# Second bias of the experts in two row tiles of TensorE, its rows loaded per tile, and silu placed before the next first layer

## The chip, the cores and the metric

The kernel runs on one core of a Trainium2 chip. The time is the device time of one execution in microseconds (us); smaller is better. Three runs of the kernel before took 1146.60, 1147.37 and 1149.48 us, so the median is 1147.37 us. A core has a matrix engine (TensorE, "PE" in the profile, with its weight loads as "PEld"), VectorE (DVE), ScalarE (ACT), GpSimd (POOL) and SyncE (SP), which only starts transfers here. Each has its own queue of instructions and they meet through semaphores. PE reads from SBUF and writes to PSUM, from which DVE and ACT fetch results.

## The reference

A layernorm, two graph layers over 1250 nodes and 40000 edges, a second layernorm, and then a layer of 8 experts of which each token uses two. Only this last part is touched by the change. Cut to it:

```python
# t: 1250 x 1024; D, H, E, K = 1024, 256, 8, 2
logits = silu(t @ rw1 + rb1) @ rw2 + rb2
vals, idx = top_k(logits, K)
w = softmax(logits with all but those K set to -inf)
eh = silu(einsum('td,edh->teh', t, ew1) + eb1)
eo = einsum('teh,ehd->ted', eh, ew2) + eb2      # eb2: 8 x 1024
y = t + einsum('te,ted->td', w, eo)
```

The second bias is eb2: for each expert a row of 1024 numbers that is added to every token's output of that expert.

## The kernel before

The kernel first does the graph layers (`gnn_windows`), then routing and experts (`moe`). A check of the edges decides at the end whether a general version has to run; with these inputs it doesn't.

In `moe` the tokens are sorted by expert into tiles of 128 rows. There can be up to 27 tiles; with these inputs there are 23. The list `eid` says which expert a tile belongs to, `ids` which tokens it holds, `to` where its rows are added, and `w_slot` the weight of each row. The first four tiles are planned from the first eight blocks of tokens (`plan_first`), the rest later (`plan_rest`), and the expert work of tiles 0 to 3 runs beside that second planning. All experts' weights lie in SBUF (`xw`), and an expert is picked by a register as an index.

One tile i goes through these steps:

- `gather(i)` (L1493): GpSimd fetches the 128 token rows from DRAM into one of three buffers by an indirect transfer.
- `fetch(i)` (L1504, L1505): PE turns the tile in eight 128 x 128 transposes, four to one PSUM buffer of the pool `tpp`; ScalarE copies each buffer of four to SBUF. The pool has two buffers.
- `first_layer(i, xT)` (L1516, L1521): eight float32 matmuls give 128 x 256 hidden values in PSUM; each shows as two passes in the profile. VectorE copies them to `hx`. Here the expert's number is also read into registers of PE and ScalarE.
- `second_layer(i, e, hx)`: two transposes turn `hx` (L1528, into a `tpp` buffer), ScalarE adds the first bias and applies silu to each half (L1530), and then each half of the 1024 output columns gets its own PSUM buffer of the pool `mm2`: a bias matmul (L1537), then two float32 matmuls (L1541, again two passes each). ScalarE scales the first half by the row weights (L1547), VectorE the second (L1549). GpSimd then adds the rows to `out` in DRAM by an indirect transfer (L1552), called the scatter below.

The bias matmul multiplies a 3 x 128 matrix of ones (`ones_b`, bfloat16) by 3 x 512 numbers: eb2 was split into three bfloat16 parts whose sum is the float32 value, and the parts were stored in DRAM as `eb2_d` of 3 x 8192. Before the experts begin, ScalarE's queue loads all of it once into three partitions of the buffer `WW` (L1624), and the matmul picks the expert's columns by PE's register.

`section(i0, i1)` sets the order in which the program is written for a run of tiles: for each i, the gather of tile i + 3, the fetch of tile i + 1, the first layer of tile i, then the second layer of tile i - 1. A planner then orders each engine's instructions: it keeps dependencies, takes instructions in program order where they are ready by its own model of times, and otherwise lets later ones that are ready go first. What `tc.keep_in_program_order` wraps is not moved that way. Tiles 0 to 19 exist always; from tile 20 on the work stands in `If` blocks that compare the number of tiles, and `sections` finishes the last tile that is held.

In `add_logits` (L1112) the router's last small matmuls already use `tile_position`: four of them with 32 columns each take four column tiles of the array.

Of the kernel before, what the change touches and what calls it, by code (L numbers as in the profile page):

```python
# [10 lines left out]
F32 = mybir.dt.float32  # L11
F32R = mybir.dt.float32r
F16 = mybir.dt.float16
BF = mybir.dt.bfloat16
# [5 lines left out]
ENG = mybir.EngineType  # L20

P = 128
# [3 lines left out]
LQ = 32  # L26
# [3 lines left out]
def kernel(  # L30
# [21 lines left out]
    nc = tc.nc  # L52
    N, D = x.shape
    NE = src.shape[0]
    E, _, H = ew1.shape
    KD = D // P
    KH = H // P
    HALF = D // 2
# [21 lines left out]
    const = ctx.enter_context(tc.tile_pool(name="const", bufs=1))  # L80
# [6 lines left out]
    eb2_d = dram.tile([3, E * D], BF, name="eb2_d")  # L87
# [7 lines left out]
    WW = L[:, NT + 4 * D :]  # L95
# [171 lines left out]
    def routing_constants():  # L267
        late = tc.keep_in_program_order
        tiles = counted(tiles_i, "tiles")
        token = counted(token_i, "token")  # L270
        own_row = counted(own_row_i, "own_row")
        first = counted(first_i, "first")
        late(nc.vector.tensor_scalar(first, first, 0.0, None, op0=ALU.is_gt))

        lower = const.tile([P, P], F16, name="lower")
        late(nc.vector.tensor_scalar(lower, lane, own_row, None, op0=ALU.is_gt))
        ones = const.tile([P, P], F16, name="ones")
        late(nc.vector.memset(ones, 1.0))
        valid = const.tile([P, NB], F32, name="valid")
        late(nc.vector.tensor_scalar(valid, token, float(N), None, op0=ALU.is_lt))  # L280

        late(nc.vector.tensor_scalar(token, token, 1.0, None, op0=ALU.add))
        late(nc.vector.tensor_mul(token, token, valid))
        rb1_p = const.tile([P, KD], F32, name="rb1_p")
        late(nc.sync.dma_start(out=rb1_p, in_=rb1.rearrange("(k p) -> p k", p=P)))

        rb2_p = const.tile([P, 1], F32, name="rb2_p")
        late(nc.vector.memset(rb2_p, 0.0))
        late(nc.sync.dma_start(out=rb2_p[:E], in_=rb2.rearrange("(e o) -> e o", o=1)))
        eb1_p = const.tile([P, E, KH], F32, name="eb1_p")  # L290
        late(nc.sync.dma_start(out=eb1_p, in_=eb1.rearrange("e (k p) -> p e k", p=P)))
        rw2_sb = const.tile([P, KD, LQ], F32, name="rw2_sb")
        late(nc.vector.memset(rw2_sb, 0.0))
        late(nc.sync.dma_start(out=rw2_sb[:, :, :E], in_=rw2.rearrange("(k p) e -> p k e", p=P)))

        ev = L[: E * D // P, NT - 320 : NT]
        eb2_f = ev[:, :P]
        late(nc.sync.dma_start(out=eb2_f, in_=eb2.rearrange("e (a n) -> (e a) n", n=P)))
        for i in range(3):
            part = ev[:, P + i * (P // 2) : P + (i + 1) * (P // 2)].bitcast(BF)  # L300
            late(nc.vector.tensor_copy(part, eb2_f))
            if i < 2:
                late(nc.vector.tensor_tensor(eb2_f, eb2_f, part, ALU.subtract))
            late(nc.sync.dma_start(out=eb2_d[i].rearrange("(a n) -> a n", n=P), in_=part))
        ones_b = const.tile([3, P], BF, name="ones_b")
        late(nc.vector.memset(ones_b, 1.0))
        lg = const.tile([P, NB, E], F32, name="lg")
        late(nc.vector.memset(lg, 0.0))
        need.update(
            tiles=tiles, token=token, first=first, lower=lower, ones=ones, valid=valid,  # L310
            rb1_p=rb1_p, rb2_p=rb2_p, eb1_p=eb1_p, rw2_sb=rw2_sb, ones_b=ones_b, lg=lg,
        )
# [698 lines left out]
    def moe():  # L1011
# [4 lines left out]
        rb1_p, rb2_p, eb1_p, rw2_sb, ones_b, lg = (  # L1016
            need[k] for k in ("rb1_p", "rb2_p", "eb1_p", "rw2_sb", "ones_b", "lg")
        )
# [71 lines left out]
        ids, to, eid = (keep([P, NTILE], I32) for _ in range(3))  # L1090
# [395 lines left out]

        w1_all = xw.rearrange("p (e w) -> p e w", e=E)[:, :, : KD * H]
        w2_all = xw.rearrange("p (e w) -> p e w", e=E)[:, :, KD * H :]
        eb2_r = WW.bitcast(BF)[:3, : E * D]
        eb2_e = eb2_r.rearrange("i (e d) -> i e d", e=E)  # L1490

        def gather(i):
            nc.gpsimd.indirect_dma_start(  # L1493
# [4 lines left out]
        def fetch(i):  # L1498
            xg = xgs[i % 3]
            xT = xTb[i % 2]  # L1500
            for q in range(0, KD, 4):
                pt = tpp.tile([P, 4, P], F32, name="tp")
                for k in range(4):
                    nc.tensor.transpose(pt[:, k, :], xg[:, (q + k) * P : (q + k + 1) * P], ident)  # L1504
                nc.scalar.copy(xT[:, q : q + 4, :], pt)  # L1505
            return xT

        def first_layer(i, xT):
            e = nc.values_load(
                eid[0:1, i : i + 1], engines=(ENG.PE, ENG.Activation),  # L1510
                min_val=0, max_val=E - 1,
                skip_runtime_bounds_check_because="eid is a count of experts, cut at E - 1",
            )
            ps = mm.tile([P, 512], F32, name="ps")
            for k in range(KD):
                nc.tensor.matmul(  # L1516
                    ps[:, :H], xT[:, k, :], w1_all[:, ds(e, 1), k * H : (k + 1) * H],
                    start=(k == 0), stop=(k == KD - 1),
                )
            hx = hxs[i % 2]  # L1520
            nc.vector.tensor_copy(hx, ps[:, :H])  # L1521
            return e, hx

        def second_layer(i, e, hx):
            pt = tpp.tile([P, 4, P], F32, name="tp")
            hT = hTs[i % 2]
            for q in range(KH):
                nc.tensor.transpose(pt[:, q, :], hx[:, q * P : (q + 1) * P], ident)  # L1528
            for q in range(KH):
                nc.scalar.activation(  # L1530
                    hT[:, q, :], pt[:, q, :], AF.Silu, bias=eb1_p[:, ds(e, 1), q : q + 1]
                )
            yo = yos[i % 2]
            for h in range(2):
                dc = slice(h * HALF, (h + 1) * HALF)
                ps = mm2.tile([P, 512], F32, name="ps2")
                nc.tensor.matmul(  # L1537
                    ps, ones_b, eb2_e[:, ds(e, 1), dc], start=True, stop=False
                )
                for q in range(KH):  # L1540
                    nc.tensor.matmul(  # L1541
                        ps, hT[:, q, :],
                        w2_all[:, ds(e, 1), q * D + h * HALF : q * D + (h + 1) * HALF],
                        start=False, stop=(q == KH - 1),
                    )
                if h == 0:
                    nc.scalar.activation(yo[:, dc], ps, AF.Copy, scale=w_slot[:, i : i + 1])  # L1547
                else:
                    nc.vector.tensor_scalar(  # L1549
                        yo[:, dc], ps, w_slot[:, i : i + 1], None, op0=ALU.mult  # L1550
                    )
            nc.gpsimd.indirect_dma_start(  # L1552
                out=out[:, :],
                out_offset=bass.IndirectOffsetOnAxis(ap=to[:, i : i + 1], axis=0),
                in_=yo, in_offset=None, bounds_check=N - 1, oob_is_err=False,
                compute_op=ALU.add,
            )
# [6 lines left out]
        xTs, held = {}, {}  # L1564

        def section(i0, i1, joined=True, until=None):
            for i in range(i0, i1):
                if i + 3 < NTILE and i > 1:
                    gather(i + 3)
                if i + 1 < (until or i1):  # L1570
                    xTs[i + 1] = fetch(i + 1)
                held[i] = first_layer(i, xTs.pop(i))
                if i > i0 or joined:
                    second_layer(i - 1, *held.pop(i - 1))

        def sections(i0, ends):
            last = held.pop(i0 - 1)
            if not ends:
                second_layer(i0 - 1, *last)
                return  # L1580

            joined = i0 == always
            if not joined:
                second_layer(i0 - 1, *last)
            with tc.If(n_tiles > i0) as more:
                xTs[i0] = fetch(i0)
                if joined:
                    held[i0 - 1] = last
                section(i0, ends[0], joined)
                sections(ends[0], ends[1:])  # L1590
            if joined:
                with more.Else():
                    second_layer(i0 - 1, *last)


        w0, w1 = route_w.pop(0), route_w.pop(0)
# [24 lines left out]
        logits(LAST)  # L1621
        lgp.close()
        mm2 = st.enter_context(tc.tile_pool(name="mmy", bufs=3, space=PSUM))
        nc.scalar.dma_start(out=eb2_r, in_=eb2_d[:, :])  # L1624
        xTs[0] = fetch(0)
        xTs[1] = fetch(1)
        held[0] = first_layer(0, xTs.pop(0))
# [14 lines left out]

    gnn_windows()
    ok = moe()
    with tc.If(ok == 0):
        gnn_any()
        moe()
# [34 lines left out]
```

## Time and profile before

The profiled execution took 1146.48 us, and its span from the first to the last instruction is 1144.3 us. The granted TensorE clock is 0.993 on average.

| What | Number | Where |
|---|---|---|
| PE busy in 958 to 1080 us | 122.00 of 122.00 us | busy time by stretch |
| ScalarE, VectorE, GpSimd busy there | 33.63, 16.46, 36.01 us | same |
| DMA engines' busy share there | 0.53 | same |
| L1516, one pass of the first layer | 384 ns, 368 of them | costliest groups |
| L1541, one pass of the second layer | 597 ns, 184 of them | same |
| L1537, one bias matmul | 379 ns, 46 of them | that line's instructions |
| L1530, silu of one half | 364 ns, 46 of them | same |
| L1505, copy of four transposes | 586 ns, 46 of them | same |
| L1552, scatter: issue to landing | 4.6 / 6.0 / 7.1 us (least, median, most) | same |

A record of a matmul lasts longer than the array is occupied[...]; the step from one start to the next is what counts. "PEld" with an idle time in brackets is a weight load that came later than the one before ended; after "<-" stands what is thought to have released it, and "issue" means that the profile shows no cause.

### The profile page before, as it was taken

To read this page: it belongs to the slowest core of one execution; us is meant where nothing else is said; L and a number is where in the kernel's file an instruction comes from. 1 tells how busy PE (TensorE), PEld (TensorE's weight loads), DVE (VectorE), ACT (ScalarE), POOL (GpSimd) and SP (SyncE) were. 2 spreads that over 40 slices of the span, in tenths; PEclk is the share of its full clock that TensorE was granted. 3 is DMA by queue.
4 is the path that set the end of the run, shared out by engine and by line. 5 is a ranking of instruction groups with operands and counts; after the bars stand their busy time and mean duration, and the time that the engine had idled before them with its cause. 6 is when DMAs were issued, how large, how long until landed. Compare 5 with 4: busy or idle time off the path is not lost.

```text
span 1144.3 us, 13214 instructions
## 1 busy us (share of the span) xinstructions
PE 1108.3 (97%) x4775; PEld 791.2 (69%) x4775; DVE 451.1 (39%) x1129; ACT 181.5 (16%) x420; POOL 331.7 (29%) x438
## 2 busy tenths in 40 slices
PE   6999999999999999999999999999999989999994
PEld 4556556888888886887688778885444766666662
DVE  8777777761212154341224132555322542111110
ACT  5301000001111111100110000123011223222220
POOL 1899999800000000032003002342000013223221
PEclk9999999999999999999999999999999999999997
DMA  6110111010100021042004261335921435444542
GB/s 230 34 38 5 38 38 38 1 37 1 38 1 1 1 74 38 1 154 93 7 10 168 88 222 42 117 148 209 373 60 37 150 92 136 112 113 105 127 115 45
DMA packets 59330, 95.40 MB, mean 83 GB/s; under 512 B 8797, under 2 KB 35645, under 8 KB 59251
## 3 DMA queue, kind: packets, MB, share of 16 engines
q1 hardware_dynamic: 48400, 67.72, 17.3%
q0 software_dynamic: 7056, 23.88, 9.2%
q10 hardware_dynamic: 3798, 2.84, 0.8%
q8 instruction: 42, 0.69, 0.2%
q14 instruction: 34, 0.28, 0.1%
HBM read 68.76 MB, written 27.47 MB: 84 GB/s over the span
## 4 chain that ended last, share of the span: by engine, by line
PE 93%; DVE 2%; ACT 1%; DMA 1%; POOL 1%; issue 0%; ACTq 0%; DVEq 0%; POOLq 0%
PE ps L528 12%; PE ps L462 11%; PE psb L642 9%; PE ps L712 8%; PE ps L564 8%; PE ps L642 7%; PE ps L1516 7%; PE ps L1541 7%; PE ps L1188 5%; PE ps L629 5%; PE ps L1202 4%; PE cnt L423 3%; PE tp L1504 2%; PE ps L1141 2%; PE ps L1537 1%; PE tp L322 1%
## 5 line engine op out<-in xcount | busy, mean ns | idle before, releaser
L413 POOL TENSOR_SCALAR ol<-lane,keys 125x128 f16<-125x128 f16 x320 | 193.2, 622 | 27.6 <-DVE oh L420 27.6
L462 PE MATMUL ps<-h0T,L 128*128 128x498 f32 (+2 forms) x384 | 147.4, 518 | 0.2 <-ACT h0T L325 0.2
L528 PE MATMUL ps<-L,h0T 128*128 128x256 f32 (+1 forms) x640 | 142.0, 380 | 0.0
L708 POOL TENSOR_TENSOR L<-L 128x512 f32<-128x512 f32 (+1 forms) x20 | 31.4, 1576 | 375.1 <-DMA L<-in_L_gnn_b_dram 216.5
L528 PEld LDWEIGHTS ps<-L,h0T 128*128 128x128 f32 (+1 forms) x640 | 118.7, 188 | 17.7 <-issue 0.5
L420 DVE TENSOR_SCALAR oh<-win,keys 125x240 f16<-125x240 f16 x320 | 84.7, 322 | 32.7 <-PE cnt L423 31.1
L462 PEld LDWEIGHTS ps<-h0T,L 128*128 128x128 f32 x384 | 68.1, 192 | 38.3 <-issue 33.9
L1516 PE MATMUL ps<-xw,L 128*128 x368 | 84.9, 384 | 0.4 <-issue 0.4
L1541 PE MATMUL ps<-xw,L 128*128 x184 | 83.5, 597 | 0.1
L564 PE MATMUL ps<-C,yh 128*128 128x256 f32 (+2 forms) x240 | 81.9, 356 | 0.0
L564 PE MATMUL ps<-C,yl 128*128 128x256 f32 (+2 forms) x240 | 81.5, 354 | 0.0
L712 PE MATMUL ps<-zh,C 128*128 128x512 f32 (+1 forms) x200 | 79.6, 398 | 0.0
L712 PE MATMUL ps<-zl,C 128*128 128x512 f32 (+1 forms) x200 | 78.7, 393 | 0.0
L1516 PEld LDWEIGHTS ps<-xw,L 128*128 128x128 f32 x368 | 69.2, 193 | 10.3 <-issue 1.8
L1552 POOL DMA_INDIRECT out_dram<-L x23 | 36.3, 1579 | 133.5 <-ACT L L1505 87.9
L442 DVE TENSOR_TENSOR C<-C,cnt 128x240 f32 x160 | 64.3, 402 | 12.5 <-DVE oh L420 1.6
L1493 POOL DMA_INDIRECT L<-t_d,L x26 | 26.0, 1000 | 148.1 <-DVE L L141 127.8
L1541 PEld LDWEIGHTS ps<-xw,L 128*128 128x128 f32 x184 | 33.3, 190 | 35.3 <-issue 32.9
L423 PEld LDWEIGHTS <-ol 125*128 125x128 f16 x320 | 30.9, 97 | 36.7 <-POOL ol L413 20.0
L1549 DVE TENSOR_SCALAR L<-ps,L 128x512 f32<-128x512 f32 x23 | 17.3, 751 | 91.8 <-PE ps L1541 91.8
L394 DVE TENSOR_TENSOR yl<-ps,yh 128x256 fp32r<-128x256 f32 (+1 forms) x40 | 16.9, 424 | 92.1 <-ACT yh L393 92.1
L423 PE MATMUL cnt<-oh,ol 125*128 125x240 f16 x320 | 50.0, 266 | 2.6 <-POOL ol L413 2.1
(226 smaller groups left out, 1504.3 us busy)
## 6 DMA issues: line engine op xcount, KB each, us to landing
xw<-in_L_ffn_ew_dram SPq DMA_DIRECT2D x16, 1024.0 KB, 7.6
L<-in_x_dram SPq DMA_DIRECT2D x20, 256.0 KB, 2.8
v_d<-L SPq DMA_DIRECT2D x18, 256.0 KB, 2.0
xa<-v_d SPq DMA_DIRECT2D x18, 256.0 KB, 6.0
t_d<-L SPq DMA_DIRECT2D x9, 512.0 KB, 4.0
out_dram<-xa SPq DMA_DIRECT2D x9, 512.0 KB, 3.7
L<-in_L_gnn_W_self_dram SPq DMA_DIRECT2D x4, 1024.0 KB, 5.4
L<-in_L_gnn_W_neigh_dram SPq DMA_DIRECT2D x4, 1024.0 KB
```

Of the source, the lines that this page charges most:

```text
L413: nc.gpsimd.tensor_scalar(ol[:, c, :], lane[:GP], keys[:, 1, c, r : r + 1], None, op0=ALU.is_equal)
L420: nc.vector.tensor_scalar(oh, win[:GP], keys[:, 0, i * GC + c, r : r + 1], None, op0=ALU.is_equal)
L423: nc.tensor.matmul(ps[:, i, :GW], ol[:, i * GC + c, :], oh, start=(c == 0), stop=(c == GC - 1),)
L442: nc.vector.tensor_tensor(to, to.bitcast(F32), ps[:, i, :GW].rearrange("p (k w) -> p k w", k=NB), ALU.add,)
L462: nc.tensor.matmul(ps[:, :n], w[:, k, (d % 2) * P : (d % 2 + 1) * P], h0T[:, k, c0 : c0 + n], start=(k == 0), stop=(k == KD - 1),)
L528: nc.tensor.matmul(ps[:m, :QW], hT[:, k, blk(b)], w[:, k, :], start=(k == 0), stop=(k == KD - 1))
L564: nc.tensor.matmul(ps[:, :n], part[: rows[k], k, (d % 2) * P : (d % 2 + 1) * P], C[: rows[k], k, c0 : c0 + n], start=(k == 0 and part is y ...
L629: nc.tensor.matmul(ps[:m], hT1[:, k, blk(b)], w[:, k, :], start=(k == 0), stop=(k == KD - 1))
L642: nc.tensor.matmul(ps, rows_of(k), w[:, k, :], start=(first and k == 0), stop=(k == KB - 1), skip_group_check=not first,)
L712: nc.tensor.matmul(ps[:m], C[: rows[k], k, blk(b)], part[: rows[k], k, :], start=(k == 0 and part is yh), stop=(k == NB - 1 and part is yl),)
L1516: nc.tensor.matmul(ps[:, :H], xT[:, k, :], w1_all[:, ds(e, 1), k * H : (k + 1) * H], start=(k == 0), stop=(k == KD - 1),)
L1541: nc.tensor.matmul(ps, hT[:, q, :], w2_all[:, ds(e, 1), q * D + h * HALF : q * D + (h + 1) * HALF], start=False, stop=(q == KH - 1),)
```

## The change

Three things are done. First, `second_layer` is split: the transposes of the hidden rows and the silus become `turn_hidden`, and `section` writes them ahead of the next tile's first layer. Second, the two bias matmuls of a tile are written one directly after the other, kept in program order, in front of both halves of the second layer, and each gets a row tile of the array: the first has its three rows in partitions 0 to 2, the second in partitions 32 to 34. `LQ` is 32. `ones_b` therefore has 35 partitions. Third, the bias rows are no longer loaded once for all experts. `load_bias(i)` has SyncE read tile i's expert into a register and load its 3 x 512 numbers for each half to one of four fixed places; the matmul then needs no register.

```diff
@@ -302,7 +302,7 @@
             if i < 2:
                 late(nc.vector.tensor_tensor(eb2_f, eb2_f, part, ALU.subtract))
             late(nc.sync.dma_start(out=eb2_d[i].rearrange("(a n) -> a n", n=P), in_=part))
-        ones_b = const.tile([3, P], BF, name="ones_b")
+        ones_b = const.tile([LQ + 3, P], BF, name="ones_b")
         late(nc.vector.memset(ones_b, 1.0))
         lg = const.tile([P, NB, E], F32, name="lg")
         late(nc.vector.memset(lg, 0.0))
@@ -1486,8 +1486,19 @@
 
         w1_all = xw.rearrange("p (e w) -> p e w", e=E)[:, :, : KD * H]
         w2_all = xw.rearrange("p (e w) -> p e w", e=E)[:, :, KD * H :]
-        eb2_r = WW.bitcast(BF)[:3, : E * D]
-        eb2_e = eb2_r.rearrange("i (e d) -> i e d", e=E)
+
+        ebs = [WW.bitcast(BF)[:, i * HALF : (i + 1) * HALF] for i in range(4)]
+
+        def load_bias(i):
+            e = nc.values_load(
+                eid[0:1, i : i + 1], engines=(ENG.SP,), min_val=0, max_val=E - 1,
+                skip_runtime_bounds_check_because="eid is a count of experts, cut at E - 1",
+            )
+            for h in range(2):
+                nc.sync.dma_start(
+                    out=ebs[i % 4][h * LQ : h * LQ + 3],
+                    in_=eb2_d[:, ds(e * D + h * HALF, HALF)],
+                )
 
         def gather(i):
             nc.gpsimd.indirect_dma_start(
@@ -1521,7 +1532,7 @@
             nc.vector.tensor_copy(hx, ps[:, :H])
             return e, hx
 
-        def second_layer(i, e, hx):
+        def turn_hidden(i, e, hx):
             pt = tpp.tile([P, 4, P], F32, name="tp")
             hT = hTs[i % 2]
             for q in range(KH):
@@ -1530,13 +1541,20 @@
                 nc.scalar.activation(
                     hT[:, q, :], pt[:, q, :], AF.Silu, bias=eb1_p[:, ds(e, 1), q : q + 1]
                 )
+            return e, hT
+
+        def second_layer(i, e, hT):
             yo = yos[i % 2]
-            for h in range(2):
+            pss = [mm2.tile([P, 512], F32, name="ps2") for _ in range(2)]
+            for h, ps in enumerate(pss):
+                tc.keep_in_program_order(
+                    nc.tensor.matmul(
+                        ps, ones_b[h * LQ : h * LQ + 3], ebs[i % 4][h * LQ : h * LQ + 3],
+                        start=True, stop=False, tile_position=(h * LQ, 0),
+                    )
+                )
+            for h, ps in enumerate(pss):
                 dc = slice(h * HALF, (h + 1) * HALF)
-                ps = mm2.tile([P, 512], F32, name="ps2")
-                nc.tensor.matmul(
-                    ps, ones_b, eb2_e[:, ds(e, 1), dc], start=True, stop=False
-                )
                 for q in range(KH):
                     nc.tensor.matmul(
                         ps, hT[:, q, :],
@@ -1568,21 +1586,29 @@
                 if i + 3 < NTILE and i > 1:
                     gather(i + 3)
                 if i + 1 < (until or i1):
+                    load_bias(i + 1)
                     xTs[i + 1] = fetch(i + 1)
+                if i > i0 or joined:
+                    turned = turn_hidden(i - 1, *held.pop(i - 1))
                 held[i] = first_layer(i, xTs.pop(i))
                 if i > i0 or joined:
-                    second_layer(i - 1, *held.pop(i - 1))
+                    second_layer(i - 1, *turned)
 
         def sections(i0, ends):
             last = held.pop(i0 - 1)
+
+            def end_of_last():
+                second_layer(i0 - 1, *turn_hidden(i0 - 1, *last))
+
             if not ends:
-                second_layer(i0 - 1, *last)
+                end_of_last()
                 return
 
             joined = i0 == always
             if not joined:
-                second_layer(i0 - 1, *last)
+                end_of_last()
             with tc.If(n_tiles > i0) as more:
+                load_bias(i0)
                 xTs[i0] = fetch(i0)
                 if joined:
                     held[i0 - 1] = last
@@ -1590,7 +1616,7 @@
                 sections(ends[0], ends[1:])
             if joined:
                 with more.Else():
-                    second_layer(i0 - 1, *last)
+                    end_of_last()
 
 
         w0, w1 = route_w.pop(0), route_w.pop(0)
@@ -1621,7 +1647,8 @@
         logits(LAST)
         lgp.close()
         mm2 = st.enter_context(tc.tile_pool(name="mmy", bufs=3, space=PSUM))
-        nc.scalar.dma_start(out=eb2_r, in_=eb2_d[:, :])
+        load_bias(0)
+        load_bias(1)
         xTs[0] = fetch(0)
         xTs[1] = fetch(1)
         held[0] = first_layer(0, xTs.pop(0))
```

## The prediction

> **What bounds the kernel now.** I read the busy shares and the chain that ended last first, then that chain over the expert tiles, then the timeline of one tile, then the tail. On the page:
>
> ```profile
> PE 1108.3 (97%) x4775; PEld 791.2 (69%) x4775; DVE 451.1 (39%) x1129; ACT 181.5 (16%) x420; POOL 331.7 (29%) x438
> ...
> PE 93%; DVE 2%; ACT 1%; DMA 1%; POOL 1%; issue 0%; ACTq 0%; DVEq 0%; POOLq 0%
> ```
>
> TensorE (PE) is the chain for 93% of the span, so what is taken from PE in an expert tile is worth its full length, unless another chain is just behind. The 23 expert tiles run from 920 us to the end. One tile from the middle (columns: start, us, what), chain view:
>
> ```profile
> 1046.44 3.46 PE ps L1516 x16
> 1049.90 0.22 PE tp L1528 x2
> 1050.12 0.53 PE ps L1537 x2
> 1050.65 0.26 PE tp L1504
> 1050.90 3.44 PE ps L1541 x8
> 1054.34 0.76 PE tp L1504 x7
> ```
>
> The period is 8.67 us (1046.44 to 1055.11), all of it PE. It holds the first layer (16 passes, 3.46), two transposes of the hidden rows (0.22), the two bias matmuls L1537, one early transpose of the next token tile, the second layer (3.44) and the other seven transposes (0.76). Timeline of the same place in an earlier tile, and, as the last line, of one weight load in a later tile (columns: start, us, engine, line, operation; in brackets the idle time before and what released it):
>
> ```profile
> 998.04 0.60 PE L1537 MATMUL ps<-L,ones_b 3*128 x2
> 998.22 0.62 ACT L1530 ACTIVATE L<-tp,eb_p 128x128 f32<-128x128 f32 x2 [3.05 <-PE tp L1528]
> 998.57 0.14 PEld L1504 LDWEIGHTS tp<-ident,L 128*128 128x128 f32 x1 [0.42 <-ACT L L1530]
> 998.74 3.60 PE L1541 MATMUL ps<-xw,L 128*128 x8
> ...
> 1076.58 0.14 PEld L1504 LDWEIGHTS tp<-ident,L 128*128 128x128 f32 x1 [0.42 <-issue]
> ```
>
> A bias record lasts 0.379 us and two make 0.60, so the second starts 0.22 after the first: 0.22 each of the array's time. The weight load behind them idles 0.42 whether its releaser is named as silu or as "issue": that gap is the second bias matmul and about 0.1 of changing over, not a wait for ScalarE. The reader is to see that silu (0.36 for the first half) already hides behind the bias pair and one transpose.
>
> **The bias pair in two row tiles.** Removed: the second 0.22 of each pair, if the two run beside each other. No row of this trace has two row tiles. The nearest has four column tiles, the router's logits:
>
> ```profile
> 872.69 1.07 PE L1112 MATMUL lg<-L,rw_sb 128*32 128x512 f32 x8
> 873.69 0.70 PE L1188 MATMUL ps<-xw 128*128 128x512 f32 x1
> ```
>
> Eight passes of 0.43 (the step of L1541, 3.44 / 8) would take 3.44 one after the other; they take 1.00 with the changes of mode at both ends, that is two rounds: fully side by side. The ends for the pair are thus no gain (0.43) and full overlap (0.22). The Trainium skill, "TensorE: Matmul & The Clock Gate", Part 3 (measured speedup), gives 3.07 times for four row tiles, not four; an estimate from it for two, at the same share of the ideal (1.54), makes the pair 0.28, which would cost 0.06 x 17 tiles = 1.0 us of the sum below. I take the row, 0.22, since column tiles of this trace overlap fully.
>
> A rule that speaks against the change is in the skill's "TensorEngine Tiling (Array Packing)", Tiling Modes (key properties): changing the tiling mode drains TensorE. If the 3-row matmuls ran in the whole-array mode before, the change would add two drains. The logits row shows such a drain: the last product ahead of it starts at 872.17 in the timeline, and 872.17 + 0.43 to 872.69 leaves 0.09; behind it some 0.13. But the bias matmuls of before have the same edges: 0.09 us between the transposes' end (997.95) and 998.04, and 0.10 from 998.47 to 998.57. So the drain is already paid; I add nothing. By the rule with two new drains it would be +0.2 x 17 = 3.4 us, and the gain would be gone.
>
> **Silu ahead of the first layer.** The two hidden transposes go ahead of 16 passes of L1516, so silu is done some 3 us before L1541 needs it. What this frees in the middle tiles is nothing by itself; it is cover. With the pair shortened, 0.22 + 0.1 would no longer hide a silu that begins 0.18 after the pair does. In tiles without a filling transpose silu does end last:
>
> ```profile
> 1085.30 0.30 PEld L1541 LDWEIGHTS ps<-xw,L 128*128 128x128 f32 x2 [0.48 <-ACT L L1530]
> ```
>
> 0.48 against 0.42 elsewhere: 0.06 each. I expect the filler to go back among its seven fellows, as PE no longer idles there. Then bias start to the third L1541 load is 1.13 (1084.71 to 1085.84) - 0.22 - 0.06 = 0.85, plus 0.11 for the transpose elsewhere = 0.96, against 1.13 (998.04 to 999.17) now: 0.17 saved; with the filler kept, 0.22. I take 0.19.
>
> The moved transposes need one of the two "tp" buffers in PSUM, and just ahead of them the fetch of the next tile fills both. A buffer is freed by ScalarE's copy:
>
> ```profile
> 1002.76 1.07 ACT L1505 COPY L<-tp 128x512 f32<-128x512 f32 x2 [1.41 <-PE tp L1504]
> ```
>
> Seven transposes start at 1002.18; with all eight there, the first copy (0.59) would end 1.28 after the group's start, the group 0.87: 0.41 apart. One L1516 matmul (two passes, 0.43) fits exactly. The order that the planner makes interleaves what is ready (10 passes of L1516, then L1541, then the other 6 around 945 to 954), so I expect one to three such matmuls ahead of the hidden transposes and take no wait; the ends are 0 and 0.5 us a tile.
>
> On ScalarE the silus move past no scaled copy of the second layer that is due earlier (L1547 runs at 1000.66, the fetch copies at 1002.76, silu then at about 1004). The tables stay as they are: silu to exp and back happens once around 934 to 946 and exp sits outside the moved stretch.
>
> **Rows loaded for each tile.** Gone: one 48 KB load issued by ScalarE at 918.15 (0.51, ScalarE idle until 920.67) and 46 address computations of 55 ns on PE's sequencer, which runs ahead; nothing on the path. Added: on SP one register load and two DMAs of 3 x 1 KB a tile. SP's queue has nothing else in this stretch (its timeline is empty). PE's bias matmul now waits for those DMAs; behind it stand eight L1541 passes. Rows of four buffers turn, so the load for tile i+1 can start when tile i-3's bias is done, over 20 us early; the nearest small transfer of SP, 16 KB to eb2_d, lands in 1.7 us. Tile 0's is issued at 918 for a use at about 928. Cost: 0; without that cover each late tile would show its lateness whole. The ones tile's larger memset (0.165 us at 114 us) costs nothing.
>
> **Where the bias was free.** At tile 1 and half of tile 2, three bias matmuls sit at 939.0 in a PE pause that lasts until 942.26 (the planning on VectorE). Tile 19's pair fills a pause at 1097.7. The new pair is held in program order and may come after those pauses.
>
> **The tail.** Each scatter to out waits for the one before:
>
> ```profile
> 1124.95 6.67 DMA out_dram<-L
> ...
> 1132.40 1.55 POOL L1552 DMA_INDIRECT out_dram<-L  x1 [5.89 <-DMA out_dram<-L]
> ```
>
> The last tile's rows were ready at 1128.53, its scatter went at 1132.40. A link is 6.67 + 0.79 = 7.46; the links before are 7.94 (1109.18 to 1117.12) and 7.83. So behind tile 19 no more than 0.48 + 0.37 = 0.85 can be won, whatever PE saves.
>
> **Sum**, against the profiled run's 1146.48 us (span 1144.3 and 2.2 around it): tile 0 -0.2; tile 1 +0.3 (0 to +0.5); tile 2 nil; tiles 3 to 16, 14 x 0.19 = -2.7 (2.3 to 3.0); tiles 17 and 18, 2 x (0.22 + 0.06) = -0.55; tile 19 +0.1 (-0.1 to +0.3); tiles 20 to 22 -0.7 (0.5 to 0.85). Together -3.7 (-2.5 to -4.6). The median shown is 1147.37, 0.9 above the profiled run; the same difference gives **1143.7 us**, own range 1142.7 to 1145.
>
> **Rivals.** (1) Slower: the hidden transposes stand directly behind the fetch and wait for the copy, 0.41 and a weight load of 0.05 to 0.1, say 0.45, in 16 tiles: +7.2 - 3.7 = +3.5, 1150.9. For it: two buffers for three uses in a row. Against it: the planner's interleaving. It decides from 0.2 us a tile, where the gain is eaten. (2) The same with one matmul between, 0.1 a tile: -2.1, 1145.3. (3) The row tiles do not overlap, so the change does not do what it says: 14 x 0.05 for the lost filler, +0.5 at tile 1, +0.3 at tile 19, -0.06 x 4: about +1.2, 1148.6. Against it: the logits row. (4) The planner's new order also closes part of the pauses around 939 or 1097: 2 more, 1141.8.
>
> **How the numbers follow.** 0.3% (3.4 us) is about what a measurement of this kernel can tell from no change. Forecast 0.48, of it 0.30 beyond 0.3% and 0.18 within; (4) 0.07, faster; (2) 0.13 and (3) 0.06, same; (1) 0.26, slower. Faster 0.37, same 0.37, slower 0.26. The likeliest case is the forecast, 1143.7; the range to 8 in 10 reaches over (2), (3) and half of (1): 1142 to 1151.
>
> **What would show it.** Right: the two L1537 records of a tile start within some 10 ns; the period in the middle falls to about 8.48; L1541's weight load is never released by silu; the last scatter still waits for the one before. Wrong: an idle before L1528 released by L1505 in every tile (rival 1 or 2); L1537 records 0.22 apart (rival 3); a gap of more than 0.1 before L1537 or after it; an idle before L1537 released by a DMA.

## The result

The changed kernel took 1150.61 us (median of 15 runs, 1149.16 to 1153.64) against 1146.81 us before (15 runs, 1145.57 to 1149.48): ratio 1.0035, 95% interval 1.0027 to 1.0043. It is slower by 3.8 us, where 3.7 us less than the 1147.37 us known then was forecast. From the page of the changed kernel, in the order shown of before (busy times, then shares of the chain):

```profile
PE 1110.2 (97%) x4775; PEld 788.7 (69%) x4775; DVE 451.4 (39%) x1129; ACT 182.3 (16%) x420; POOL 331.5 (29%) x438
...
PE 94%; DMA 2%; DVE 1%; ACT 1%; POOL 1%; issue 0%; SPq 0%; DVEq 0%; POOLq 0%; ACTq 0%
```

Nothing in these totals tells where the time is. The chain over the middle tiles (3 to 17) does, since it has two kinds of tile where before had one. In the changed kernel L1515 are the fetch's transposes, L1539 the hidden ones, L1527 the first layer, L1551 the bias pair, L1559 the second layer, L1516 ScalarE's copy (start, us, what):

```profile
1003.26 0.87 PE tp L1515 x8
1004.13 0.43 PE ps L1527 x2
1004.57 0.30 PE tp L1539 x2
1004.86 3.02 PE ps L1527 x14
1007.89 0.32 PE ps L1551 x2
1008.21 3.63 PE ps L1559 x8
...
1038.35 0.45 PE tp L1515 x4
1038.88 0.59 ACT L L1516
1039.48 0.04 issue
1039.52 0.44 PE tp L1539 x2
1039.96 0.07 issue
1040.03 3.71 PE ps L1527 x16
1043.74 0.32 PE ps L1551 x2
1044.06 3.63 PE ps L1559 x8
```

In the first kind one first-layer matmul (two passes) stands between the fetch and the hidden transposes, and the tile takes 8.58 us. In the second there is none, ScalarE's copy is on the chain, and the tile takes 9.34 us. Both are to be held against 8.67 before. The two kinds split the middle: tiles 3 to 10 are of the first, 11 to 17 of the second. Timed by the ends of VectorE's scaled copy, one per tile, and counted from the last logits (VectorE, L1242), so that the runs' differences in the untouched part drop out:

| Stretch | before | after | difference |
|---|---|---|---|
| last logits to tile 2 (planning beside tiles 0 to 2) | 40.65 | 40.71 | +0.06 |
| tiles 3 to 10 | 69.23 | 68.66 | -0.57 |
| tiles 11 to 17 | 60.66 | 65.40 | +4.74 |
| tiles 18 and 19 | 18.23 | 17.63 | -0.60 |
| tile 19 to the end | 36.28 | 36.68 | +0.40 |
| sum | 225.05 | 229.08 | +4.03 |

Seven tiles, 11 to 17, are the whole loss. The first row holds some luck: in these two profiled runs TensorE's clock stood at half for about 6.8 us of the planning stretch in the changed kernel and 3.4 in before (the last section has the working). The timeline of one of the seven:

```profile
1029.53 1.08 ACT L1516 COPY L<-tp 128x512 f32<-128x512 f32 x2 [1.52 <-PE tp L1515]
1030.17 0.20 PEld L1539 LDWEIGHTS tp<-ident,L 128*128 128x128 f32 x2 [0.53 <-ACT L L1516]
...
1030.68 1.38 PEld L1527 LDWEIGHTS ps<-xw,L 128*128 128x128 f32 x7 [0.31 <-issue]
```

The hidden transposes' weight load waits 0.53 until the copy has freed a "tp" buffer, and then the first layer's loads come another 0.31 late with no cause that the profile names. The line that reads the expert's number (L1520) has one, for two of these tiles (least, median and longest time in ns, then first and last start):

```profile
L1520 PEldq TENSOR_LOAD <-L x2: 301/305/309, 1030.2 to 1039.5; - x2
```

PE's sequencer, which issues its instructions ("PEldq"), reads the register only from 1030.2 on, when the transposes have been let go, and the first layer's loads need it. In a tile of the first kind it is read during the second layer ahead (at 1008.2, for a first layer that starts at 1012.71).

### The profile page after: what moved, and what is told of

It reads as the page before. It is cut to its first block, busy times and chain, and to the rows that moved or that the text cites. A ratio compares the mean times of both kernels' runs of the same rounds, so it can differ in the third digit from the quotient of the medians.

```text
span 1149.5 us, 13379 instructions
## 1 busy us (share of the span) xinstructions
PE 1110.2 (97%) x4775; PEld 788.7 (69%) x4775; DVE 451.4 (39%) x1129; ACT 182.3 (16%) x420; POOL 331.5 (29%) x438
## 4 chain that ended last, share of the span: by engine, by line
PE 94%; DMA 2%; DVE 1%; ACT 1%; POOL 1%; issue 0%; SPq 0%; DVEq 0%; POOLq 0%; ACTq 0%
PE ps L528 12%; PE ps L462 12%; PE psb L642 9%; PE ps L712 8%; PE ps L564 8%; PE ps L642 7%; PE ps L1527 7%; PE ps L1559 7%; PE ps L1188 5%; PE ps L629 5%; PE ps L1202 4%; PE cnt L423 3%; PE ps L1141 2%; PE tp L1515 2%; DMA L<-in_L_gnn_W_self_dram 1%; PE tp L788 1%
## 5 line engine op out<-in xcount | busy, mean ns | idle before, releaser
L1527 PE MATMUL ps<-xw,L 128*128 x368 | 88.2, 387 | 0.7 <-issue 0.3
L1559 PE MATMUL ps<-xw,L 128*128 x184 | 85.0, 605 | 0.2 <-ACT L L1541 0.2
L1527 PEld LDWEIGHTS ps<-xw,L 128*128 128x128 f32 x368 | 68.1, 193 | 10.9 <-issue 2.8
L1559 PEld LDWEIGHTS ps<-xw,L 128*128 128x128 f32 x184 | 33.1, 189 | 38.3 <-issue 37.8
L141 DVE TENSOR_TENSOR L<-L,ps 128x512 f32<-128x512 f32 (+1 forms) x28 | 17.1, 611 | 86.9 <-PE ps L1188 44.7
```

What stands on the lines that cost most here:

```text
L1527: nc.tensor.matmul(ps[:, :H], xT[:, k, :], w1_all[:, ds(e, 1), k * H : (k + 1) * H], start=(k == 0), stop=(k == KD - 1),)
L1559: nc.tensor.matmul(ps, hT[:, q, :], w2_all[:, ds(e, 1), q * D + h * HALF : q * D + (h + 1) * HALF], start=False, stop=(q == KH - 1),)
```

## The experiments

Two theories were set against each other: (A) the place of the hidden transposes in the seven tiles is the loss; (B) the row loads, the waits for them or the row tiles cost something in every tile. "Before" in the ratios is the kernel before, measured on the same chip beside each.

**The register read one tile earlier.** Only the place in the program moves; the planner then puts one matmul between in all middle tiles.

```diff
                 if i + 1 < (until or i1):
+                    if i > 3:
+                        es[i + 1] = expert_of(i + 1)
                     load_bias(i + 1)
...
-            e = nc.values_load(
...
+            e = es.pop(i) if i in es else expert_of(i)
```

> The changed kernel, only with the expert's number of tile i read into PE's and ScalarE's registers one tile earlier; the planner then puts one first-layer matmul between the fetch and the hidden transposes in all middle tiles, where the changed kernel has seven tiles with none. Theory A (the seven tiles with the hidden transposes directly behind the fetch are the loss, 9.34 us against 8.58 each): 7 x 0.76 = 5.3 us off, 1145.3 us, 1.5 below before, and every middle tile at 8.58. Rival B (row loads on SP, waits for them, or row tiles cost something spread over all tiles): still about 1150.

Measured: 1145.80 us, ratio 0.9984 (0.9977 to 0.9991). All fifteen middle tiles take 8.58. One that was of the slow kind:

```profile
1025.96 0.87 PE tp L1515 x8
1026.83 0.43 PE ps L1532 x2
1027.27 0.30 PE tp L1544 x2
1027.56 3.02 PE ps L1532 x14
1030.59 0.32 PE ps L1556 x2
```

The changed kernel with nothing but this other order is faster than before, so A stands, and B is not the loss: the loads of SP, the waits for them and the row tiles are all still there. What in the slow order costs the time, the place, the wait or the late read, this run doesn't tell; the next three do.

**Hidden transposes held behind the third first-layer matmul.** They and the first layer's matmuls are kept in program order.

```diff
             for k in range(KD):
+                if k == 3 and between is not None:
+                    between()
-                nc.tensor.matmul(
+                tc.keep_in_program_order(nc.tensor.matmul(
...
-                    turned = turn_hidden(i - 1, *held.pop(i - 1))
-                held[i] = first_layer(i, xTs.pop(i))
+                    held[i] = first_layer(
+                        i, xTs.pop(i), lambda: turned.append(turn_hidden(i - 1, *before))
+                    )
```

> The changed kernel with the hidden transposes written by hand behind the third of the eight first-layer matmuls and kept there. Theory A: no wait for the copy in any tile, so 8.50 us a tile in the middle (the 8.58 less the 0.08 that the transposes wait with one matmul ahead): 1144 us, 2.5 to 3 below before. Rival B: about 1150.

Measured: 1146.27 us, ratio 0.9993 (0.9985 to 1.0002). The middle tiles are at 8.50 as expected, but the planning stretch came out longer: tile 2 ends at 41.70 after the last logits instead of 40.65 in before, and PE's pause there lasts 5.10 us instead of 2.43, since the pinned work is not moved into it. Part of what the middle gained, the order by hand took away at the start.

**Hidden transposes held directly behind the fetch in every tile** (`k == 0` instead of `k == 3` above).

> The changed kernel with the hidden transposes kept directly ahead of the first layer in every tile, that is directly behind the fetch. Theory A: 9.34 in all 15 middle tiles instead of 8.50 with three matmuls between: 15 x 0.84 = 12.6 us over that kernel's 1146.3, 1159. If only some tiles paid (something else of tiles 11 to 17): about 1152.

Measured: 1156.83 us, ratio 1.0083 (1.0067 to 1.0098). Every middle tile pays, but 9.01, not 9.34: 15 x (9.01 - 8.50) = 7.7 of the 10.6 us over the kernel pinned at 3; 2 more are in the planning stretch (43.75 against 41.70). The size was wrong, and the reason shows in its timeline:

```profile
1008.20 0.20 PEld L1544 LDWEIGHTS tp<-ident,L 128*128 128x128 f32 x2 [0.53 <-ACT L L1516]
1008.37 3.32 PEld L1530 LDWEIGHTS ps<-xw,L 128*128 128x128 f32 x16
```

The wait for the copy is the same 0.53, but the first layer (L1530 here) follows at once, without the 0.31. In this kernel PE reads the expert's register ahead of the hidden transposes (at 1003.4 here); in the changed kernel's seven tiles it reads it behind them. So 0.84 = 0.51 for the buffer + 0.33 for the read that was held up behind the waiting instruction.

**A PSUM buffer of its own for the hidden transposes**, taken from the three of the second layer.

```diff
-            pt = tpp.tile([P, 4, P], F32, name="tp")
+            pt = turnp.tile([P, 4, P], F32, name="th")
...
-        mm2 = st.enter_context(tc.tile_pool(name="mmy", bufs=3, space=PSUM))
+        mm2 = st.enter_context(tc.tile_pool(name="mmy", bufs=2, space=PSUM))
+        turnp = st.enter_context(tc.tile_pool(name="turnp", bufs=1, space=PSUM))
```

> The changed kernel with a PSUM buffer of its own for the hidden transposes, taken from the three of the second layer. The planner puts them directly behind the fetch in every tile. Theory A in its finer form (not the place but the wait for the shared buffer costs): no wait, 8.50 us a tile, 1144 us. If the place itself costs (change of work on PE, the register read queued behind them): 9.0 or more a tile, above 1152.

Measured: 1140.48 us, ratio 0.9940 (0.9926 to 0.9954). This beats both kernels. Chain of one of its tiles:

```profile
1003.56 3.63 PE ps L1559 x8
1007.19 0.87 PE tp L1515 x8
1008.07 0.22 PE th L1539 x2
1008.28 3.46 PE ps L1527 x16
1011.74 0.32 PE ps L1551 x2
```

The transposes stand directly behind the fetch, the register read stands behind them in the program, and the tile takes 8.50: the place and the read cost nothing when nothing waits (the read starts at 1003.8, over 4 us ahead of its use). But the kernel is 3.5 us below what was expected; tile 2 ends at 36.70 after the logits, 3.95 earlier than before.

**The same buffer in the kernel before**, with nothing of the change.

> The kernel before, nothing of the change, with a PSUM buffer of its own for the hidden transposes (two left for the second layer). If the gain of the own buffer beyond 8.50 a tile lies in the planning stretch (no pause of PE while VectorE plans, so no drop of the granted clock to 0.50 behind it): the middle tiles stay at 8.67, the planning stretch is some 4 us shorter, 1143 us. Then the change itself is worth 1143 - 1140.5 = 2.5 us where the buffer is not short. If the own buffer only removes the wait that the change brought: 1147.

Measured: 1143.02 us, ratio 0.9960 (0.9946 to 0.9974). Middle tiles 8.67, tile 2 at 36.40. So some 4 us belong to the buffer in the planning stretch: tile 1's hidden transposes start there at 939.84 and its second layer follows, where in before they start at 944.20, behind the planning's own matmuls into a "tp" buffer (L1359). The change on top of the buffer is worth 1143.02 - 1140.48 = 2.5 us; the two were measured on different chips, and by their ratios to before it is 0.0020, 2.3 us.

**Silu put back behind the next first layer**, row tiles and row loads kept.

```diff
-                if i > i0 or joined:
-                    turned = turn_hidden(i - 1, *held.pop(i - 1))
                 held[i] = first_layer(i, xTs.pop(i))
                 if i > i0 or joined:
-                    second_layer(i - 1, *turned)
+                    second_layer(i - 1, *turn_hidden(i - 1, *held.pop(i - 1)))
```

> Row tiles and rows per tile kept, silu put back behind the next first layer, as before. If the pair was only shortened under a silu that then ends last: L1541 cannot start before about 0.85 us after the hidden transposes began, as in before, so 8.6 to 8.67 us a tile and 1146 to 1147 us, no gain. If silu does not set that start: 8.67 - 0.22 = 8.45 a tile, 1143 us. Rival B: above 1149.

Measured: 1148.87 us, ratio 1.0019 (1.0011 to 1.0026). The middle tiles are at 8.66: the shorter pair buys nothing when silu ends last. The chain there, then silu and the second layer's first weight load from the timeline:

```profile
1007.37 0.22 PE tp L1539 x2
1007.59 0.32 PE ps L1551 x2
1007.91 0.26 PE tp L1515
1008.17 3.64 PE ps L1559 x8
...
1007.69 0.62 ACT L1541 ACTIVATE L<-tp,eb_p 128x128 f32<-128x128 f32 x2 [3.05 <-PE tp L1539]
1008.11 0.30 PEld L1559 LDWEIGHTS ps<-xw,L 128*128 128x128 f32 x2
```

The first half's silu takes 0.36 and so ends at 1008.05; the load of its result follows at 1008.11. Before, eight passes of the second layer took 3.44 on the chain behind such a transpose; here 3.64: what the pair gave up, 0.53 to 0.32, came back as a late start. The 2 us over before come from the planning stretch (41.83 against 40.65) and the tail (37.15 against 36.28), and were not expected. In the planning stretch the profiled run had TensorE at half clock for about 6.8 us where before had 3.4, which by the estimate of the last section is 1.3 us; the tail is open.

**Both bias matmuls in one row tile.** Each half's rows get a place of their own in partitions 0 to 2.

```diff
-                        ps, ones_b[h * LQ : h * LQ + 3], ebs[i % 4][h * LQ : h * LQ + 3],
-                        start=True, stop=False, tile_position=(h * LQ, 0),
+                        ps, ones_b[:3], ebs[i % 4 * 2 + h][:3],
+                        start=True, stop=False, tile_position=(0, 0),
```

> The changed kernel with both bias matmuls in the same row tile (partitions 0 to 2), everything else and PE's order alike. If the two row tiles run beside each other, this costs 0.216 us more in some 19 tiles whose pair is on the path: about 1154.7. If they ran one after the other already: 1150.6, as the changed kernel.

Measured: 1156.56 us, ratio 1.0082 (1.0066 to 1.0097). The tiles are at 8.79 and 9.56 where the changed kernel has 8.58 and 9.34, and the pair shows as

```profile
1007.70 0.53 PE ps L1551 x2
```

instead of 0.32. The second row tile saves 0.21 of the 0.22 by which two bias matmuls start apart in before. The time is 1.9 us above the expected 1154.7; the profiled run took 1154.92, and what the other three spent more on is open.

**Silu ahead of the first layer alone**, on the kernel before.

```diff
+            return e, hT
+
+        def second_layer(i, e, hT):
...
+                if i > i0 or joined:
+                    turned = turn_hidden(i - 1, *held.pop(i - 1))
                 held[i] = first_layer(i, xTs.pop(i))
                 if i > i0 or joined:
-                    second_layer(i - 1, *held.pop(i - 1))
+                    second_layer(i - 1, *turned)
```

> The kernel before with only the silus written ahead of the next first layer; bias rows loaded once, no row tiles. The planner puts each bias matmul in front of its own half, and the hidden transposes directly behind the fetch in 6 middle tiles, behind one first-layer matmul in 9. If each change to the small matmul and back costs about 0.3 (0.09 before, 0.1 after and a weight load that shows): 9.10 and 9.86 us a tile, some 11 over before, 1158. If going into the row mode costs nothing by itself: 8.7 and 9.5, about 1152.

Measured: 1159.40 us, ratio 1.0101 (1.0085 to 1.0117); tiles 9.09 and 9.85. Its chain shows two bias matmuls that nothing holds together:

```profile
1009.62 0.32 PE ps L1540
1009.93 1.91 PE ps L1544 x4
1011.85 0.32 PE ps L1540
1012.16 1.91 PE ps L1544 x4
```

With silu early the planner puts each before its own half. Two single ones cost 9.09 - 8.79 = 0.30 more than two in a row: that is what one more change to the three-row matmul and back costs. This kernel too has six tiles of the slow kind, so the slow order comes from the moved silu and not from the row loads.

## Why the prediction was wrong

**What bounds, the pair, the drain: right.** The pair fell from 0.53 to 0.32 on the chain, and the one-row-tile kernel shows the 0.21 directly. The timeline has the two records, 0.384 us each, in 0.39 together, where before had 0.60, so they start within about 0.01:

```profile
1007.82 0.39 PE L1551 MATMUL ps<-L,ones_b 3*128 3x512 bf16 x2
```

The row of the column tiles was the right guide: full overlap. The estimate from the Trainium skill's "TensorE: Matmul & The Clock Gate", Part 3 (0.28 for the pair) was too pessimistic here. The drain at a change of tiling mode that the Trainium skill states ("TensorEngine Tiling (Array Packing)", Tiling Modes) fits the 0.30 that one more change and back costs in the kernel with silu alone (how much of it is drain is not shown). It was already paid before, as argued: the pair on the chain is its streaming and about 0.1 in both kernels (0.53 with two steps of 0.22, 0.32 with one).

**Silu as cover: right.** Without it the middle tiles stay at 8.66.

**Tiles with the buffer free: right in size.** 8.50, that is 0.17 saved, at the lower end of 0.17 to 0.22, since the filling transpose did go back to its fellows.

**The step that failed** is "I expect one to three such matmuls ahead of the hidden transposes and take no wait". The planner put one ahead in tiles 3 to 10 (a wait of 0.08 each) and none in tiles 11 to 17; what was put at nothing cost 8 x 0.08 + 7 x 0.84 = 6.5 us. Its end of "0.5 us a tile" was too low as well: the seven paid 0.84, since the register read behind the waiting transposes was not counted. To name what is queued behind the waiting instruction would have found it: the read stands in the same queue. Rival (1) had the mechanism and, at 1150.9, nearly the time, but by 16 tiles at 0.45 instead of seven at 0.84; that the two sums meet is chance. (Rival (4) should read 1141.7; nothing hangs on it.)

**Why seven and not all or none** is open in part. The planner decides by its own model of times, and the two orders must be nearly level in it, since moving a register read by one tile turned all seven. What tips it at tile 11 was not tried.

**Smaller terms.** Tiles 0 to 2: +0.1 expected in sum, +0.06 measured, with the longer stretch at half clock in it; by the estimate of the last section the changed kernel would be 1.3 ahead there without that. The tail was to give 0.7 and took 0.4: the last three links between scatters are 8.59, 7.62 and 7.39 against 7.94, 7.83 and 7.45. The first is longer because tile 19's scatter, which starts it, left sooner after its rows (0.80 against 1.16), and because tile 20 takes 8.58 instead of 8.27: all eight transposes of its fetch now stand in its own time (0.87 on the chain, 0.44 before). That the last link is a transfer was right:

```profile
1129.83 6.61 DMA out_dram<-L
```

**The row loads: nothing,** as expected; no bias matmul waited for one.

## What to carry to other kernels

When work is moved forward, list the buffers that it takes at its new place and who frees them: here three users of two PSUM buffers came to stand in a row, and 0.51 us a tile was lost by that alone. What stood behind the waiting instruction was held up with it, here a register read for 0.33 more, so the price of a wait is the wait plus what could have run ahead. Where a planner orders the work by its own clock, look at the order it made in every tile, not in one, or take away the shared buffer so that the order doesn't matter.

## What was not expected of the hardware

TensorE's granted clock fell to half around a pause of 2.43 us in the planning stretch. All eight kernels with such a pause there (2.40 to 6.51 us) show the fall, and the two with the own buffer, which have no pause at that place, don't. Busy time by stretch, for before and then for the changed kernel with its own buffer (us of each engine with counts, then granted clock, DMA share, GB/s):

```profile
core 0: us, PE busy (x) PEld busy (x) DVE busy (x) ACT busy (x) POOL busy (x), PEclk, DMA share, GB/s
939.00:942.00 3.00, 0.83 (x4) 0.30 (x4) 2.93 (x12) 0.00 (x0) 0.00 (x0) 1.00 0.97 149
942.00:944.00 2.00, 1.65 (x28) 1.41 (x27) 1.47 (x10) 0.72 (x2) 0.60 (x1) 0.94 0.22 43
944.00:946.00 2.00, 2.00 (x7) 1.47 (x7) 1.79 (x8) 1.56 (x3) 1.39 (x3) 0.50 0.37 76
946.00:948.00 2.00, 2.00 (x8) 1.63 (x7) 1.88 (x6) 1.01 (x3) 1.18 (x1) 0.71 0.93 350
```

```profile
939.00:942.00 3.00, 3.00 (x12) 1.62 (x11) 2.86 (x15) 0.00 (x0) 0.59 (x1) 1.00 0.68 82
942.00:944.00 2.00, 2.00 (x27) 1.08 (x26) 1.55 (x6) 1.57 (x2) 0.00 (x0) 1.00 0.71 141
944.00:946.00 2.00, 2.00 (x13) 1.45 (x12) 1.27 (x5) 1.44 (x4) 1.43 (x2) 1.00 0.11 21
```

In before PE is busy for 0.83 of three microseconds, resumes at 942.26, and runs at half clock while it is fully busy again. With the own buffer the second layer of tile 1 fills the pause and the clock stays at 1.00.

How long the clock stays down differs between runs. From the share granted, before has it at half for (0.06 x 2 + 0.50 x 2 + 0.29 x 2) / 0.5 = 3.4 us; the changed kernel for 6.8:

```profile
942.00:944.00 2.00, 1.11 (x23) 1.11 (x23) 1.50 (x7) 0.22 (x1) 0.00 (x0) 0.55 0.53 106
944.00:946.00 2.00, 2.00 (x10) 1.48 (x9) 1.73 (x10) 1.13 (x2) 1.63 (x2) 0.50 0.14 22
946.00:948.00 2.00, 2.00 (x5) 1.59 (x6) 1.90 (x8) 1.96 (x4) 1.54 (x2) 0.50 0.79 279
948.00:950.00 2.00, 2.00 (x7) 1.49 (x6) 0.61 (x1) 0.00 (x0) 0.00 (x0) 0.74 0.89 266
```

The kernel with the earlier register read has PE's work in the same order up to tile 2, but 3.4 us at half clock, and ends tile 2 at 39.38 after the logits instead of 40.71. So 3.4 us at half clock cost about 1.3 us there. By this estimate some 1.3 of the 4 us of the own-buffer kernels are the kept clock and the rest the filled pause; they were not measured apart.

The Trainium skill states the rule in "TensorE: Matmul & The Clock Gate", Part 1: after an idle window of some 3.4 us the array is clocked at half. The trace agrees on the half; the pauses of before and of the changed kernel (2.82) were shorter than that. By the shares granted, the fall came at 943.76 in before, 1.5 us after work had resumed, and at 942.2 in the changed kernel, ahead of PE's return at 942.89.
